# A convolution, attention and expert kernel: key deviations by Newton's steps, a new layout of the shifted rows, and new places in the slots

## The chip, the cores and the metric

The kernel runs on one core of one Trainium2 chip. A core has five engines with a queue of instructions each: TensorE (PE in the profile, its weight loads PEld), VectorE (DVE), ScalarE (ACT), GpSimd (POOL) and SyncE (SP), which here only starts DMAs. The metric is the device time of one execution in microseconds; lower is better. A matmul writes to PSUM, of which this kernel uses eight banks; everything else lies in SBUF (128 partitions) or in DRAM.

## The reference

The input x has 8 images of 56 x 56 positions with 256 channels, 25,088 tokens in all. Cut to what matters:

```python
# layer 0: 32 paths, each 256 -> 4 -> 3x3 conv -> 4 -> 256
h = relu(bn1(x @ w1 + b1)); h = relu(bn2(conv3x3(h, w2) + b2)); h = relu(bn3(h @ w3 + b3))
x = relu(sum_over_paths(h) + x)
# layer 1 on tokens t
q = layernorm(t)                                        # eps 1e-5
k = (q_head - mean) / (std(ddof=1) + 1e-5)              # per head of 32 channels; v likewise
kv = k^T v / N;  attn = q @ kv + q;  t = t + attn
z = layernorm(t)
moe = z + sum over the two best of 8 experts of weight * (gelu(z @ w1 + b1) @ w2 + b2)
out = t + moe
```

The deviations of the change's name are the std of each head and the deviation of the layer norm in front of it.

## The kernel before

The tokens are cut into S = 56 chunks of 448 tokens (8 rows of an image; NCH = 7 chunks an image). The program is a pipeline over slots s = 0, 1, ...; a slot brings together different stages of different chunks:

- conv3 of chunk s (lines 586 to 639): 16 step pairs. A pair makes two products on PE for two groups of paths (line 596, tile `c`); ACT takes one with bias and relu into a tile `r` (601), DVE takes the other and adds it into `r` (604). Every second step PE sums four of the `r` over the paths with a 0/1 matrix `gather` (617, tile `su`). There are 7 buffers of `r` and 7 PSUM banks for all products.
- conv1 of chunk s + 2 and conv2 of chunk s + 1 (255 to 339). conv2 reads `R`, the first layer's rows shifted by 0, 1 and 2 columns, which three DMAs of line 298 bring into 96 partitions; its weights `W2t` are laid out to match. Its result, split into high and low halves, goes to `hl` by DMAs (333).
- `end_steps` of chunk s - 1 (645): relu, transposes, then the keys: means per head on DVE, `center` on POOL (690), squares on ACT (699), `variances` on DVE (708 to 727) and the root of 36 values a partition by POOL's power (728), `inverse` on DVE (736 to 742), `scale` on POOL (746), and the products k^T v on PE (756).
- attention of chunk a = s - 8 (862), with its second layer norm (DVE statistics, a power on POOL at 900, or a Newton iteration on DVE at 916 for the last chunks, called alone), and its base result to the output (943).
- routing of two chunks at a time (969): scores, the two best experts, ranks, and scatters of rows into regions of DRAM by POOL (1073). At certain chunks a plan (1099) is made on DVE: which 256 rows of which expert form a tile.
- expert tiles (1252 to 1402): SP reads row and expert numbers, loads the rows `z` (1266) and the weights `w` (1276); PE transposes (1287), ACT copies, DVE copies the routing weight into `g` (1294) and the row numbers into `index` (1298); PE and ACT do the two layers (1329 to 1353), the second scaled by `g`; POOL adds the result into the output by an indirect DMA (1367).

There are 210 expert tiles. The slots have three eras: up to slot 7 only the convolution and the end steps run; from slot 8 attention and routing join; from slot 18 on tiles join. After slot 55 a tail is left, which has the last attention, routing and tiles.

The order of the work on PE, ACT and DVE is that of the program. Each step of a stage has a place between 0 and 1 in its slot, from the table `places` (1410), or it is spread evenly between two bounds; `issue` (1438) sorts a slot's steps by place and emits them. SP's and POOL's orders are left to the scheduler of the framework. `tiles_by` (1455) says how many tiles are done by each slot; its list `after` is for the slots past the last chunk.

The lines that the power and what follows it stand on:

```python
            nc.vector.tensor_scalar_mul(sd[:, :, :NH], ss, 1.0 / (HC - 1))
            nc.gpsimd.tensor_tensor(
                sd, sd, half[:T, :].rearrange("q (k h) -> q k h", k=KT), ALU.pow
            )
```

Of the kernel before, what the change touches and what calls it, by code (L numbers as in the profile page):

```python
# [8 lines left out]
F32 = mybir.dt.float32  # L9
# [16 lines left out]
def kernel(  # L26
# [165 lines left out]
    def whole(parts_of, name):  # L192
# [96 lines left out]
    def spread_taps(s):  # L289

        b, c = divmod(s, NCH)
        R = taps.tile([3 * 32, NG, TL], F32, tag="R", name=f"R_{s}")
        flat = h1.rearrange("p r w -> p (r w)")
        r0 = c * ROWS * W58
        for dx in range(3):
            n = TL - dx
            queue = nc.scalar if s == 0 and dx == 1 else nc.sync
            queue.dma_start(
                out=R[32 * dx : 32 * dx + 32, :, :n], in_=flat[:, r0 + dx : r0 + dx + n]
            )  # L300
        tapped[s] = R
# [119 lines left out]
    for f in range(NF):  # L421
        tp = ps_mm.tile([P, 512], F32, tag="mm", name=f"tp_sb_{f}")
        nc.tensor.transpose(tp[:, :NP], bias3[:, f * P : (f + 1) * P], ident[:NP, :NP])
        b3T = setup.tile([P, NP], F32, name=f"b3T_{f}")
        nc.scalar.copy(b3T, tp[:, :NP])
        nc.vector.tensor_reduce(sumb[:, f, :], b3T[:, NP // 2 :], AX.X, ALU.add)
    setup_pool.__exit__(None, None, None)
# [67 lines left out]

    b2hl = const.tile([P, C], F32R, name="b2hl")
    b2s = const.tile([P, C], F32, name="b2s")
    b2l = const.tile([E, C], F32R, name="b2l")
    nc.gpsimd.memset(b2s, 0.0)
    nc.sync.dma_start(out=b2s[:E], in_=b2)  # L500
    nc.vector.tensor_copy(b2hl, b2s)
    nc.vector.tensor_tensor(b2l, b2s[:E], b2hl[:E].bitcast(F32), ALU.subtract)
    nc.sync.dma_start(out=b2hl[E : 2 * E].bitcast(F32), in_=b2l.bitcast(F32))
# [79 lines left out]

    unit, sums = {}, {}
# [44 lines left out]
    def conv3_steps(s):  # L629
        steps = []  # L630
        units = NF * NQ
        for step in range(0, 4 * units, 2):
            if is_chunk(s):
                steps.append((0.7, lambda step=step: (pair(s, step), pair(s, step + 1))))
            if step == 0 and is_chunk(s - 1):
                steps.append((0.9, lambda: sum_paths(s - 1, units - 1)))
            if step and step % 4 == 0 and is_chunk(s):
                steps.append((0.9, lambda step=step: sum_paths(s, step // 4 - 1)))
        return steps
# [4 lines left out]

    def end_steps(s):
        b, c = divmod(s, NCH)
        v = {}

# [55 lines left out]
        def variances():  # L704
# [23 lines left out]
            nc.gpsimd.tensor_tensor(  # L728
                sd, sd, half[:T, :].rearrange("q (k h) -> q k h", k=KT), ALU.pow
            )  # L730

        def inverse():

            sd = v["sd"]
            inv = v["inv"] = small([T, KT, NH], "hinv")
            nc.vector.scalar_tensor_tensor(
                inv, sd[:, :, NH:].to_broadcast([T, KT, NH]), HEAD_EPS, sd[:, :, :NH],
                op0=ALU.mult, op1=ALU.add,
            )
# [122 lines left out]
    def attn_steps(a):  # L862
# [15 lines left out]
        def attend(k):  # L878
# [16 lines left out]
            if k == KT - 1:  # L895
                nc.vector.tensor_scalar_add(rs2, mv[:, :, 1], LN_EPS)
                if alone:
                    inverse_root(rs2)
                else:
                    nc.gpsimd.tensor_tensor(rs2, rs2, mhalf[:T, :KT], ALU.pow)  # L900
# [14 lines left out]

        def inverse_root(t):

            v, y, h = (
                stat.tile([T, KT], dt, tag=f"root{n}", name=f"root{n}_{a}", bufs=1)
                for n, dt in enumerate((F32, I32, F32))  # L920
            )
            nc.vector.tensor_copy(v, t)
            nc.vector.tensor_scalar(y, t.bitcast(I32), 1, None, ALU.arith_shift_right)
            nc.vector.tensor_scalar(y, y, -1, 0x5F3759DF, ALU.mult, ALU.add)
            y = y.bitcast(F32)
            for _ in range(4):
                nc.vector.scalar_tensor_tensor(h, y, -0.5, v, op0=ALU.mult, op1=ALU.mult)
                nc.vector.tensor_mul(h, h, y)
                nc.vector.scalar_tensor_tensor(y, h, 1.5, y, op0=ALU.add, op1=ALU.mult)
            nc.vector.tensor_copy(t, y)  # L930
# [321 lines left out]
    def empty_rows(e):  # L1252
        pad = slots.tile([P, 2, ROW], F32, tag="rows", name=f"pad_{e}")
# [27 lines left out]
    def tile_in(i):  # L1281
# [10 lines left out]

        g = slots.tile([P, 2], F32, tag="g", name=f"g_{i}")
        nc.vector.tensor_copy(g, z[:, :, C + k])  # L1294
# [92 lines left out]
    def moe_steps(first, last):  # L1387
# [20 lines left out]


    places = {  # L1410
        "attention": [0.108, 0.243, 0.378, 0.514, 0.622, 0.689, 0.744, 0.798, 0.881, 0.881],
        "attention first": [0.396, 0.487, 0.578, 0.669, 0.742, 0.834, 0.87, 0.907, 0.943, 0.989],
        "conv1": [0, 0, 0.111],
        "conv1 alone": [0, 0.011, 0.024],
        "conv2": [0.615, 0.615, 0.625, 0.675],
        "conv2 alone": [0.636, 0.642, 0.642, 0.79],
        "end": [0.109, 0.16, 0.22, 0.251, 0.346, 0.44, 0.56, 0.69, 0.77, 0.917],
        "end alone": [0.125, 0.16, 0.17, 0.23, 0.31, 0.39, 0.39, 0.64, 0.734, 0.869],
        "fetch": [0.099],
        "image": [0.012, 0.118, 0.225],  # L1420
        "plan": [0.432, 0.95],
        "route": [0.016, 0.368],
        "scatter": [0.302, 0.63],
        "taps": [0.144],
        "taps alone": [0.373],
    }

# [27 lines left out]
    def tiles_by(s):  # L1455
# [3 lines left out]
        after = [8, 5, 5, 5, 6, 5, 5, 5, 10]  # L1459
# [10 lines left out]
    for s in range(S + A + 1):  # L1470
# [17 lines left out]
        if is_chunk(a):  # L1488
# [3 lines left out]
            if a + A > S:  # L1492
                work_of.append((0.35 if opens else 0.05, 0.97, attn_steps(a)))
            else:
                work_of.extend(at("attention first" if opens else "attention", attn_steps(a)))
        work_of.extend(left)
        left = []
        if waiting and (len(waiting) == 2 or waiting[-1] % NCH == NCH - 1):
            last_image = waiting[-1] >= S - NCH
            compute, scatters = route_steps(waiting)  # L1500
            work_of.append((places["route"][0], places["route"][1], compute))
            if last_image:
                work_of.append((0.35, 1.0, sum(scatters, [])))
# [8 lines left out]
        if r >= 0 and r + 1 < len(closing):  # L1512
# [3 lines left out]
            work_of.append((0.0 if s > known_in[r] else 0.2, 1.0, moe_steps(upto, goal)))  # L1516
# [69 lines left out]
```

## Time and profile before

| | us |
|---|---|
| median of 3 runs | 3239.76 |
| lowest, highest | 3237.83, 3244.07 |
| profiled execution | 3252.06 |
| its span in the profile | 3250.3 |
| PE, DVE, ACT, POOL busy | 2947.0, 2222.2, 1923.3, 1900.3 |

The mean granted clock of TensorE was 0.959 of full speed. The profile comes from one execution and gives for each engine when each instruction ran, what ended the idle time before it, and for PE the granted clock. Line numbers are those of the kernel before. A line of a group reads: line, engine, operation, output and input tiles, shapes, count, busy us, mean ns of one, and the idle time in front with what ended it. A line of waits reads: who waited for whom, us in total, times, longest. In a timeline the two first numbers are the start and the length in us, and the bracket at the end is the idle time before it. A PE that is busy isn't a PE at its peak, since the ends of matmuls are modelled.

### The profile page before, as it was taken

The page shows a single profiled execution, that of the slowest core. Times are in us where ns is not written, and L with a number is a line of the kernel's source. Part 1 is how long each engine was busy: PE and PEld are TensorE (multiplying, and loading weights), DVE is VectorE, ACT ScalarE, POOL GpSimd, SP SyncE. Part 2 cuts the span into 40 slices and gives each one's busy share as a digit, 9 for nine tenths or more (in the row PEclk, how much of TensorE's full clock was granted, in tenths as well). Part 3 has the DMA queues.
Part 4 walks back from the last instruction along what each step waited for, and adds up shares of the span by engine and source line. Part 5 has one row for each costly group of instructions (what it writes and reads, how often), then busy time and mean ns, then how long its engine had stood idle before and what let it go on. Part 6 is the DMA issues. An engine that isn't in the chain of part 4 may idle for free. (4 is left out here: it accounts for less than half of the span.)

```text
span 3250.3 us, 53680 instructions
## 1 busy us (share of the span) xinstructions
PE 2947.0 (91%) x16677; PEld 1672.9 (51%) x16677; DVE 2222.2 (68%) x5887; ACT 1923.3 (59%) x3827; POOL 1900.3 (58%) x1372
## 2 busy tenths in 40 slices
PE   4999888888999999999899999999999998988798
PEld 2343444333454545555455555555555545776687
DVE  3778877787878787776877787877778775434210
ACT  2676655556666656566566666566666654444355
POOL 3223244445556665746656665666655757777677
PEclk7999998899999999999999999999999999989899
DMA  8442454455566766667666666667566756899797
GB/s 163 120 107 80 113 130 125 118 148 145 153 168 167 191 151 176 165 171 199 163 163 171 181 166 180 172 169 191 157 186 164 182 154 173 200 241 222 185 230 172
DMA packets 322670, 537.54 MB, mean 165 GB/s; under 512 B 41152, under 2 KB 232784, under 8 KB 322384
## 3 DMA queue, kind: packets, MB, share of 16 engines
q1 hardware_dynamic: 238272, 429.85, 46.7%
q0 software_dynamic: 81984, 103.45, 17.4%
q8 instruction: 133, 2.18, 0.3%
q10 hardware_dynamic: 2128, 0.81, 0.1%
q14 instruction: 153, 1.25, 0.1%
HBM read 248.01 MB, written 192.55 MB: 136 GB/s over the span
## 5 line engine op out<-in xcount | busy, mean ns | idle before, releaser
L604 DVE SCALAR_TENSOR_TENSOR r<-c,nb,r 128x448 f32<-128x448 f32 x1792 | 1127.5, 676 | 424.2 <-ACT r L601 380.7
L601 ACT ACTIVATE r<-c,b3t 128x448 f32<-128x448 f32 x1792 | 1040.1, 634 | 351.8 <-PE c L596 321.2
L1367 POOL DMA_INDIRECT out_dram<-y,index x420 | 661.0, 1574 | 340.1 <-ACT y L1353 206.8
L596 PE MATMUL c<-hl,W3hl 64*128 64x448 f32 x3584 | 696.1, 428 | 58.3 <-ACT r L601 20.8
L1073 POOL DMA_INDIRECT regions<-pay,rrowi x448 | 430.3, 961 | 342.8 <-PE c L596 229.5
L617 PE MATMUL su<-r,gather 128*32 128x448 f32 x3584 | 567.7, 570 | 38.2 <-DVE r L604 30.6
L596 PEld LDWEIGHTS c<-hl,W3hl 64*128 64x128 f32 x3584 | 328.8, 188 | 524.7 <-issue 247.2
L1329 PE MATMUL ph<-eT,w 128*128 128x256 f32 x1680 | 466.2, 409 | 41.0 <-DVE r L604 18.6
L1349 PE MATMUL py<-w,hT 128*128 128x256 f32 x1680 | 437.5, 385 | 2.8 <-ACT hT L1333 2.7
L1353 ACT ACTIVATE y<-py,g 128x256 f32<-128x256 f32 x420 | 196.6, 475 | 387.2 <-PE py L1349 276.2
L1329 PEld LDWEIGHTS ph<-eT,w 128*128 128x128 f32 x1680 | 307.3, 198 | 179.6 <-issue 61.2
L728 POOL TENSOR_TENSOR hsd<-hsd,half 112x36 f32<-112x36 f32 x56 | 346.6, 6189 | 85.1 <-DVE hsd L727 83.1
L1333 ACT ACTIVATE hT<-ph,w 128x256 f32<-128x256 f32 x420 | 198.1, 477 | 248.3 <-PE ph L1329 127.2
L1349 PEld LDWEIGHTS py<-w,hT 128*128 128x128 f32 x1680 | 293.9, 193 | 32.5 <-ACT hT L1333 3.5
L882 PE MATMUL at<-tab,tT 128*112 128x272 f32 x896 | 260.2, 414 | 14.2 <-ACT r L601 7.7
L690 POOL TENSOR_TENSOR norm<-t,hmean 112x512 f32<-112x512 f32 x112 | 126.8, 1259 | 240.4 <-PE c L596 130.0
L617 PEld LDWEIGHTS su<-r,gather 128*32 128x32 f32 x3584 | 100.9, 109 | 246.8 <-issue 121.9
L882 PEld LDWEIGHTS at<-tab,tT 128*112 128x112 f32 x896 | 147.3, 179 | 90.2 <-issue 21.6
L1345 PE MATMUL py<-b2hl,own 128*128 128x256 f32 x420 | 178.3, 424 | 16.6 <-issue 12.6
L1291 ACT COPY eT<-te 128x512 f32<-128x512 f32 x210 | 123.9, 590 | 85.9 <-PE te L1287 63.8
L1018 POOL TENSOR_TENSOR rq<-ebase,rq 112x8 f32<-112x8 f32 (+1 forms) x32 | 52.6, 1643 | 208.1 <-DVE rq L1017 208.1
L886 DVE SCALAR_TENSOR_TENSOR X<-at,rs,X 112x256 f32<-112x256 f32 x224 | 106.7, 476 | 80.0 <-PE at L882 36.2
(255 smaller groups left out, 3241.8 us busy)
## 6 DMA issues: line engine op xcount, KB each, us to landing
w<-Wd SPq DMA_DIRECT2D x210, 513.0 KB
rows<-regions SPq DMA_DIRECT2D x210, 259.0 KB
xi<-in_x_dram SPq DMA_DIRECT2D x56, 448.0 KB
hl<-hi SPq DMA_DIRECT2D x112, 224.0 KB
tTs<-u SPq DMA_DIRECT2D x56, 448.0 KB
ts<-t SPq DMA_DIRECT2D x56, 448.0 KB
tT<-tTs SPq DMA_DIRECT2D x56, 448.0 KB
X<-ts SPq DMA_DIRECT2D x56, 448.0 KB
```

The lines of the kernel that those rows point to most:

```text
L596: product = nc.tensor.matmul(tiles[g][:, :CH], W3hl[rows, ab, cg, :], hl[rows, ab, :], start=True, stop=True)
L601: nc.scalar.activation(r, tiles[0][:, :CH], AF.Relu, bias=b3t[:, cg, 2 * ab : 2 * ab + 1])
L604: nc.vector.scalar_tensor_tensor(r, tiles[1][:, :CH], nb3[:, cg, 2 * ab + 1 : 2 * ab + 2], r, op0=ALU.max, op1=ALU.add,)
L617: nc.tensor.matmul(ps[32 * c4 : 32 * c4 + 32, :CH], gather, unit.pop((s, 4 * u + c4)), start=(ab == 0), stop=(ab == NQ - 1),)
L728: nc.gpsimd.tensor_tensor(sd, sd, half[:T, :].rearrange("q (k h) -> q k h", k=KT), ALU.pow)
L882: nc.tensor.matmul(ps, tT[:, f, k * T : (k + 1) * T], tables_of[b][:, f, :], start=(f == 0), stop=(f == NF - 1),)
L1073: ins = nc.gpsimd.indirect_dma_start(out=regions[n], out_offset=bass.IndirectOffsetOnAxis(ap=v["row_i"][:, (m - group[0]) * KT + k, n : n ...
L1329: nc.tensor.matmul(ps, w[:, f * C + hf * P : f * C + (hf + 1) * P], eT[:, f, :], start=(f == 0), stop=(f == NF - 1),)
L1333: nc.scalar.activation(hT[:, hf, :], ps, AF.Gelu, bias=w[:, 2 * NF * C + hf : 2 * NF * C + hf + 1])
L1349: nc.tensor.matmul(ps, hT[:, f, h * P : (h + 1) * P], w[:, (NF + f) * C : (NF + f + 1) * C], start=False, stop=(f == NF - 1),)
L1353: nc.scalar.activation(y[:, h, :], ps, AF.Identity, scale=g[:, h : h + 1])
L1367: ins = nc.gpsimd.indirect_dma_start(out=out_rows, out_offset=at, in_=y[:, h, :], in_offset=None, compute_op=ALU.add, **partial,).ins
```

## The change

It has five parts.

1. From chunk 8 on (`newton = s >= 8`), `variances` doesn't call POOL's power. DVE finds 1/sqrt by a bit trick and three Newton steps (`inverse_root`, eleven instructions on 112 x 36 values) and multiplies by the value to get the root; `inverse` copies the reciprocal root of the token instead of taking a reciprocal. The Newton iteration of the last chunks' second norm uses the same function, with three steps where it had four and one copy less.
2. `R` holds the three shifts of a row in neighbouring partitions: each DMA writes every third partition of 96 instead of 32 neighbouring ones. The weights `W2s` and the mask `path32` follow; the mask is made at once, without the sum of `path96`.
3. ACT scales a tile's result by the routing weight in the loaded rows `z` themselves; the copy `g` is gone. The rows have five buffers instead of four, for the empty rows of the start too.
4. The second bias `b2` is prepared at the end of the setup, in memory that is given back after it.
5. `places` has new numbers, and names for what had fixed bounds: the attention of the last chunks, the last routing and scatters, the tiles' bounds, and `after`, whose first entry is 7 for 8.

```diff
-    path96 = setup.tile([P, 3 * GP, D], F32, name="path96")
-    group_mask(path96, 3 * GP, D, 1.0)
     path32 = setup.tile([P, GP, D], F32, name="path32")
-    nc.vector.tensor_reduce(
-        path32, path96.rearrange("q (n g) d -> q g d n", n=3), AX.X, ALU.add
-    )
+    group_mask(path32, GP, 3 * D, 1.0)
...
-                out=W2s[32 * dx : 32 * dx + 32, g],
+                out=W2s[dx : 3 * 32 : 3, g],
...
-                out=R[32 * dx : 32 * dx + 32, :, :n], in_=flat[:, r0 + dx : r0 + dx + n]
+                out=R[dx : 3 * 32 : 3, :, :n], in_=flat[:, r0 + dx : r0 + dx + n]
...
+    def inverse_root(v, y, h):
+
+        nc.vector.tensor_scalar(y, v.bitcast(I32), 1, None, ALU.arith_shift_right)
+        nc.vector.tensor_scalar(y, y, -1, 0x5F3759DF, ALU.mult, ALU.add)
+        y = y.bitcast(F32)
+        for _ in range(3):
+            nc.vector.scalar_tensor_tensor(h, y, -0.5, v, op0=ALU.mult, op1=ALU.mult)
+            nc.vector.tensor_mul(h, h, y)
+            nc.vector.scalar_tensor_tensor(y, h, 1.5, y, op0=ALU.add, op1=ALU.mult)
+        return y
...
-            nc.gpsimd.tensor_tensor(
-                sd, sd, half[:T, :].rearrange("q (k h) -> q k h", k=KT), ALU.pow
-            )
+            if not newton:
+                nc.gpsimd.tensor_tensor(
+                    sd, sd, half[:T, :].rearrange("q (k h) -> q k h", k=KT), ALU.pow
+                )
+                return
+            y = stat.tile([T, KT, NH + 1], I32, tag="root1", name=f"root1_{s}", bufs=1)
+            h = stat.tile([T, KT, NH + 1], F32, tag="root2", name=f"root2_{s}", bufs=1)
+            y = v["y"] = inverse_root(sd, y, h)
+            nc.vector.tensor_mul(sd, sd, y)
...
-            nc.vector.reciprocal(rs1s[s], sd[:, :, NH])
+            if newton:
+                nc.vector.tensor_copy(rs1s[s], v["y"][:, :, NH])
+            else:
+                nc.vector.reciprocal(rs1s[s], sd[:, :, NH])
...
-        z = slots.tile([P, 2, ROW], F32, tag="rows", name=f"rows_{i}")
+        z = slots.tile([P, 2, ROW], F32, tag="rows", name=f"rows_{i}", bufs=5)
...
-        g = slots.tile([P, 2], F32, tag="g", name=f"g_{i}")
-        nc.vector.tensor_copy(g, z[:, :, C + k])
+        g = z[:, :, C + k]
...
-        "attention first": [0.396, 0.487, 0.578, 0.669, 0.742, 0.834, 0.87, 0.907, 0.943, 0.989],
+        "attention first": [0.396, 0.487, 0.578, 0.669, 0.742, 0.953, 0.953, 0.953, 0.953, 0.989],
-        "conv2": [0.615, 0.615, 0.625, 0.675],
+        "conv2": [0.615, 0.615, 0.655, 0.675],
-        "conv2 alone": [0.636, 0.642, 0.642, 0.79],
+        "conv2 alone": [0.607, 0.613, 0.613, 0.761],
-        "end": [0.109, 0.16, 0.22, 0.251, 0.346, 0.44, 0.56, 0.69, 0.77, 0.917],
+        "end": [0.109, 0.151, 0.211, 0.242, 0.337, 0.431, 0.551, 0.681, 0.761, 0.908],
-        "image": [0.012, 0.118, 0.225],
+        "image": [0.001, 0.107, 0.214],
-        "plan": [0.432, 0.95],
+        "plan": [0.569, 0.983],
-        "route": [0.016, 0.368],
+        "route": [0, 0.368],
-        "scatter": [0.302, 0.63],
+        "scatter": [0.302, 0.551],
-        "taps alone": [0.373],
+        "taps alone": [0.391],
...
-                work_of.append((0.35 if opens else 0.05, 0.97, attn_steps(a)))
+                work_of.extend(at("attention first last" if opens else "attention last", attn_steps(a)))
...
-            work_of.append((0.0 if s > known_in[r] else 0.2, 1.0, moe_steps(upto, goal)))
+            work_of.append((places["tiles"][s <= known_in[r]], places["tiles"][2], moe_steps(upto, goal)))
```

Of what is left out above: the tiles' bounds are now 0.043 (0.2 in the first slot of a round) to 0.99, the last image's routing stands at 0 to 0.254, its scatters from 0.35 to 0.995, fetch at 0.119 (0.099 before).

More of the change, by code (lines that the diff above doesn't have):

```diff
@@ L426 @@
         nc.vector.tensor_reduce(sumb[:, f, :], b3T[:, NP // 2 :], AX.X, ALU.add)
+    b2hl = const.tile([P, C], F32R, name="b2hl")
+    b2s = setup.tile([P, C], F32, name="b2s")
+    b2l = setup.tile([E, C], F32R, name="b2l")
+    nc.gpsimd.memset(b2s, 0.0)
+    nc.sync.dma_start(out=b2s[:E], in_=b2)
+    nc.vector.tensor_copy(b2hl, b2s)
+    nc.vector.tensor_tensor(b2l, b2s[:E], b2hl[:E].bitcast(F32), ALU.subtract)
+    nc.sync.dma_start(out=b2hl[E : 2 * E].bitcast(F32), in_=b2l.bitcast(F32))
     setup_pool.__exit__(None, None, None)
@@ L494 @@
     Wd = tc.dram_tile([E, P, WROW], F32, name="Wd")
[L496 to L503, printed above, removed]
     pos_i = const.tile([P, 2], I32, name="pos_i")
@@ L578, in unordered @@
         tc.declare_no_dep(ins, group=group, keep=keep, reason="other rows")
+    places = {
+        "after": [7, 5, 5, 5, 6, 5, 5, 5, 10],
+        "attention": [0.108, 0.243, 0.378, 0.514, 0.622, 0.689, 0.744, 0.798, 0.881, 0.881],
+        "attention first": [0.396, 0.487, 0.578, 0.669, 0.742, 0.953, 0.953, 0.953, 0.953, 0.989],
+        "attention last": [
+            0.151, 0.272, 0.393, 0.514, 0.611, 0.611, 0.657,
+            0.706, 0.754, 0.791, 0.815, 0.839, 0.863, 0.912,
+        ],
+        "attention first last": [
+            0.611, 0.692, 0.774, 0.856, 0.921, 0.962, 0.982,
+            0.982, 0.982, 0.982, 0.982, 0.982, 0.982, 0.982,
+        ],
+        "conv1": [0, 0, 0.111],
+        "conv1 alone": [0, 0.011, 0.024],
+        "conv2": [0.615, 0.615, 0.655, 0.675],
+        "conv2 alone": [0.607, 0.613, 0.613, 0.761],
+        "end": [0.109, 0.151, 0.211, 0.242, 0.337, 0.431, 0.551, 0.681, 0.761, 0.908],
+        "end alone": [0.143, 0.178, 0.188, 0.248, 0.328, 0.408, 0.408, 0.658, 0.752, 0.887],
+        "fetch": [0.119],
+        "image": [0.001, 0.107, 0.214],
+        "tiles": [0.043, 0.2, 0.99],
+        "conv3": [0.7, 0.9],
+        "plan": [0.569, 0.983],
+        "route": [0, 0.368],
+        "route last": [0, 0.254],
+        "scatter": [0.302, 0.551],
+        "scatter last": [0.35],
+        "taps": [0.144],
+        "taps alone": [0.391],
+    }
     unit, sums = {}, {}
@@ L633, in conv3_steps @@
             if is_chunk(s):
-                steps.append((0.7, lambda step=step: (pair(s, step), pair(s, step + 1))))
+                steps.append((places["conv3"][0], lambda step=step: (pair(s, step), pair(s, step + 1))))
             if step == 0 and is_chunk(s - 1):
-                steps.append((0.9, lambda: sum_paths(s - 1, units - 1)))
+                steps.append((places["conv3"][1], lambda: sum_paths(s - 1, units - 1)))
             if step and step % 4 == 0 and is_chunk(s):
-                steps.append((0.9, lambda step=step: sum_paths(s, step // 4 - 1)))
+                steps.append((places["conv3"][1], lambda step=step: sum_paths(s, step // 4 - 1)))
         return steps
@@ L647, in end_steps @@
         v = {}
+        newton = s >= 8
         def begin():
@@ L897, in attend @@
                 if alone:
-                    inverse_root(rs2)
+                    y, h = (
+                        stat.tile(
+                            [T, KT, NH + 1], dt, tag=f"root{n}", name=f"root{n}_{a}_a", bufs=1
+                        )[:, :, 0]
+                        for n, dt in ((1, I32), (2, F32))
+                    )
+                    nc.vector.tensor_copy(rs2, inverse_root(rs2, y, h))
                 else:
@@ L914, in normed @@
             )
[L916 to L930, printed above, removed]
         def raised(k):
@@ L1252, in empty_rows @@
     def empty_rows(e):
-        pad = slots.tile([P, 2, ROW], F32, tag="rows", name=f"pad_{e}")
+        pad = slots.tile([P, 2, ROW], F32, tag="rows", name=f"pad_{e}", bufs=5)
         nc.gpsimd.memset(pad, 0.0)
@@ L1402, in moe_steps @@
         return steps
-    places = {
-        "attention": [0.108, 0.243, 0.378, 0.514, 0.622, 0.689, 0.744, 0.798, 0.881, 0.881],
-        "attention first": [0.396, 0.487, 0.578, 0.669, 0.742, 0.834, 0.87, 0.907, 0.943, 0.989],
-        "conv1": [0, 0, 0.111],
-        "conv1 alone": [0, 0.011, 0.024],
-        "conv2": [0.615, 0.615, 0.625, 0.675],
-        "conv2 alone": [0.636, 0.642, 0.642, 0.79],
-        "end": [0.109, 0.16, 0.22, 0.251, 0.346, 0.44, 0.56, 0.69, 0.77, 0.917],
-        "end alone": [0.125, 0.16, 0.17, 0.23, 0.31, 0.39, 0.39, 0.64, 0.734, 0.869],
-        "fetch": [0.099],
-        "image": [0.012, 0.118, 0.225],
-        "plan": [0.432, 0.95],
-        "route": [0.016, 0.368],
-        "scatter": [0.302, 0.63],
-        "taps": [0.144],
-        "taps alone": [0.373],
-    }
     def at(name, steps):
@@ L1458, in tiles_by @@
         most = known_after[-2] - 2
-        after = [8, 5, 5, 5, 6, 5, 5, 5, 10]
+        after = [int(v) for v in places["after"]]
         if s >= S:
@@ L1500 @@
             compute, scatters = route_steps(waiting)
-            work_of.append((places["route"][0], places["route"][1], compute))
+            rt = places["route" if s < S else "route last"]
+            work_of.append((rt[0], rt[1], compute))
             if last_image:
-                work_of.append((0.35, 1.0, sum(scatters, [])))
+                work_of.append((places["scatter last"][0], 0.995, sum(scatters, [])))
             else:
```

## The prediction

> **What bounds the kernel now.** I read the page first (engine totals, the forty slices), then a table by stage, then who waited for whom in each stage, then a timeline of one wait. The stage borders are the first relu of line 601 of a slot: slots 0 to 7 (convolution alone) 65 to 335 us, slots 8 to 18 (attention and routing join) to 814, slots 19 to 55 (expert tiles join) to 2717, then the tail without convolution, whose last part (3124 on) has tiles only. Columns: stretch, its length, busy us of PE, its weight loads, DVE, ACT, POOL with counts, granted PE clock, DMA share, GB/s.
>
> ```profile
> PE 2947.0 (91%) x16677; PEld 1672.9 (51%) x16677; DVE 2222.2 (68%) x5887; ACT 1923.3 (59%) x3827; POOL 1900.3 (58%) x1372
> ...
> 65.00:335.30 270.30, 252.21 (x1478) 108.08 (x1476) 211.84 (x401) 181.50 (x324) 71.68 (x35) 0.99 0.42 110
> 335.30:814.40 479.10, 412.46 (x2367) 187.48 (x2366) 379.49 (x933) 284.69 (x544) 225.12 (x154) 0.93 0.49 130
> 814.40:2717.00 1902.60, 1800.09 (x10475) 982.67 (x10474) 1454.28 (x3681) 1204.23 (x2395) 1192.55 (x812) 0.98 0.66 171
> 2717.00:3124.00 407.00, 342.81 (x1665) 279.41 (x1666) 144.67 (x728) 177.23 (x413) 288.48 (x215) 0.92 0.86 212
> 3124.00:3250.00 126.00, 114.63 (x600) 100.94 (x598) 12.16 (x77) 68.85 (x142) 97.41 (x64) 0.96 0.81 194
> ```
>
> PE is 95% busy in the long third stage, so there only its gaps and its lowered clock can be won. The second stage is different: PE idles 66.6 us of 479 and the clock is lowest. The waits of DVE and PE in that stage, then in the third (us in total, times, longest):
>
> ```profile
> DVE hinv L736 <- POOL hsd L728: 26.3, 9, 4.2
> PE su L617 <- DVE r L604: 27.0, 10, 4.2
> ...
> DVE hinv L736 <- POOL hsd L728: 36.9, 30, 3.2
> PE kv L756 <- DVE r L604: 23.0, 10, 4.4
> PE ph L1329 <- DVE r L604: 18.6, 11, 2.1
> ```
>
> The two totals of the second stage are one event, as slot 10 shows: POOL's power takes 6.16 us, DVE stands 4.22 us in front of it, the relus behind stand too, and PE stands 4.21 us.
>
> ```profile
> 442.80 6.16 POOL L728 TENSOR_TENSOR hsd<-hsd,half 112x36 f32<-112x36 f32 x1
> 449.00 0.19 DVE L736 SCALAR_TENSOR_TENSOR hinv<-hsd 112x32 f32<-112x32 f32 x1 [4.22 <-POOL hsd L728]
> 450.24 1.70 PE L617 MATMUL su<-r,gather 128*32 128x448 f32 x3 [4.21 <-DVE r L604]
> ...
> 450.20:454.60 4.40, 4.36 (x13) 1.49 (x13) 2.45 (x5) 1.36 (x3) 2.75 (x3) 0.50 0.09 28
> ```
>
> The last line is the stretch after it: PE runs at half its clock. In the third stage the waits have another cause:
>
> ```profile
> L728 POOL TENSOR_TENSOR hsd<-hsd,half 112x36 f32<-112x36 f32 x56 | 346.6, 6189 | 85.1 <-DVE hsd L727 83.1 <-DVE hmu L723 0.9 <-issue 0.9
> L1294 DVE COPY g<-rows 128x2 f32<-128x2 f32 x210 | 72.5, 346 | 27.2 <-ACT y L1353 18.8 <-issue 8.4
> ...
> 1132.42 3.06 DVE L1294 COPY g<-rows 128x2 f32<-128x2 f32 x1
> 1132.80 2.65 POOL L690 TENSOR_TENSOR norm<-t,hmean 112x512 f32<-112x512 f32 x2
> 1136.20 1.13 PE L1329 MATMUL ph<-eT,w 128*128 128x256 f32 x4 [2.05 <-DVE r L604]
> ```
>
> A copy of two columns, 0.16 us in the median of 210, lasts 3.06 us while POOL centers the keys, and PE then stands 2.05 us.
>
> [...] GpSimd's power does not seem to block (the cast at line 328 took 0.38 us inside slot 10's). [...] In the trace's packet records between 1000 and 2600 us a packet of R (2,312 bytes, into 32 neighbours) has a median of 214 ns, one of 3,584 bytes for u and t 140 ns[...].
>
> **The change, part by part.**
>
> *Newton on DVE, chunks 8 to 55.* Removed: 48 powers of 6.19 us, 297 us of POOL. Added on DVE: two tensor_scalars, nine steps and a product, 12 instructions in a chain. The like-sized chain of lines 714 to 723 starts one every 0.22 us (durations 0.19), so 12 x 0.22 = 2.6 us a chunk, 48 x 2.6 = 125 us; the reciprocal of rs1 (0.12) becomes a copy (0.16), nothing. Behind the chain on DVE stand u, the relus and hi and lo; PE's sums wait for the relus. Second stage, ten chunks: the 27.0 us of PE waits go. Half clock behind them is 37.5 us by the clock records of slots 10 to 17, which lost up to 18.8 us; I take 10. Against that the chain is exposed: slot 9 has 1.8 us of idle DVE between variances and inverse to absorb 2.6, others less; exposure 0.9 to 2.6, taken as 1.5, ten times 15. Sum -22; ends -27 - 18.8 + 9 = -37 and -27 + 26 = about 0. Third stage, 37 chunks: the 36.9 us of DVE waits cost PE only 2 us by its own waits, and slots are filled by tiles, so the chain mostly runs beside ph and py: credit -5, exposure 0.2 us x 37 = +7. If that cover is gone, 2 us x 37 = +74. Sum +2; ends -15, +74. In slots 19 to 55 DVE has 448 us idle against 37 x 2.6 = 96 added.
>
> *Weights without a copy.* 210 copies go, 72.5 us of DVE, about half of it blocked time. [...] PE's ph waits are 18.6 us, and the half clock at slots 25, 27, 34, 41 and 53 is 5 x 3.41 us, costing half: 8.5. Ends -27 and 0; I take -11. The rows buffer is now held until ACT has scaled with it (line 1353), two iterations longer, with five buffers for four: taking rows n + 2 waits for output n - 3, which is the last step of the iteration before. SP's weight load n + 1 has waited for that same output all along (480.8 us of SP wait at line 1276), so SP's queue gets no new bound; rows still have two iterations of 4.1 us before they are turned. Cost 0; without the cover, up to the tail's DMA-heavy 400 us x 2%, 8 us.
>
> *Shifted rows over all partitions.* If R's packets fell to the rate of the 3,584-byte ones, 90 ns, DMA work between 1000 and 2600 would fall by 12,032 packets x (199 mean - 90) / 16 = 82 us, five points of share. No PE gap over 0.8 us in slots waits for R, and conv2 stands 0.47 of a slot (22 us) behind taps: 0, ends -8, +3. The mask in one piece saves one reduce of 0.27 us, hidden under W2's loads.
>
> *b2 into the setup.* One memset, two DMAs, two DVE instructions move ahead by a little; PE waits there for g3's DMA (10.8 us). 0.
>
> *New places.* The order of PE's instructions stays, but for the last third of conv2 (one pair-step later), the image matrix before conv1, and tiles, which start at 0.043 of a slot and come 3 or 4 a slot more evenly; one tile moves from the tail into the slots (4.1 us either way). The plan moves from 0.432-0.95 to 0.569-0.983. Its long DVE instructions were blocked behind POOL in slots 26, 33, 47 and 54 (2.76 and 2.88 us in a row in slot 26) and PE waited 4.4 us at kv each time, 23.0 us in all, with 4 x 6.83 us at half clock: 37 us at stake. Later, they meet the POOL sum X instead of the scale: I take a third, -12; ends -37, +10. Tail: PE idles 64 us of 407 before 3124, at clock 0.92. Route and attention come earlier, so scatters and last plan can too: -5; ends -40, +20 (DMA is at 0.86 there). Newton with three steps instead of four in seven tail chunks: 0.7 us each on a DVE that is 36% busy, 0.
>
> Sum: -22 + 2 - 11 - 12 - 5 = -48 us on the profiled 3252.06 us (span 3250.3): 3204. The runs' median is 3239.76, 12.3 below the profiled one: **3192 us**.
>
> **Rivals.** *More is won* (0.20): the kv and ph waits go whole and the tail fills; -37 + 2 - 27 - 30 - 20 = -112, 3128 us. For: the waits are few, with a place each. [...] *The waits only move* (0.10): [...] plan collides with the sum X, the exposed chain eats what the power's wait cost; 0 to -12, 3228 to 3240. *DVE's chain becomes the bound* (0.17), slower: variances already hold DVE 2.5 us in a row and would hold it 5.1; the relu ring has 7 buffers, and slot 9 shows a DVE hold of 2.25 us reaching PE as 2.24. At 2 us exposed in 37 slots and 2.6 in ten the sum is -48 + 67 + 11 = +30, 3270 us. It decides where the exposure exceeds my values by 1.0 us a chunk on the mean (48/47). Against: DVE is 76% busy in the third stage and PE has tiles to run. The change not taking effect is excluded for Newton, since the instructions are there; for R it is in the third rival.
>
> **How the numbers follow.** The forecast has 0.53, own range 3165 to 3222. To hold eight in ten the range takes in half of the larger gain and the moved waits and the near part of the slower case: 3140 to 3255. A measurement tells 0.2%, 6.5 us, from no change. Slower: 0.17 plus a bit of the moved waits, 0.18; same 0.05; faster 0.77.
>
> **What would show it.** No power at line 728 beyond 8; POOL about 1600 us busy; DVE about 2270 (2222 + 125 - 72.5 - 5). In the second stage the wait of su for r falls from 27 us to under 15, and the clock rises from 0.93. The L1298 copies keep a mean under 0.25 us. kv's wait in the third stage falls by a third. PE's relu waits rising in every slot after line 727's place would prove the prediction wrong, as would SP waiting for ACT at the rows load with te waiting for rows, or a tail longer than 533 us.

## The result and the profile after

The changed kernel took **3205.92 us** in the median of 4 runs (3205.22 to 3206.05), the kernel before 3240.41 beside it: a ratio of 0.9892, interval [0.9875, 0.9909]. The profiled execution took 3205.89 us, its span is 3204.2, the granted clock 0.969 in the mean. In a later group of runs (`after_b` below) the same kernel took 3236.3 beside 3247.5 us, ratio 0.9957 [0.9943, 0.9971]. The change is a gain both times, of 34 us and of 11.

The busy totals from the page of the changed kernel, and the group of the index copy before and after (columns as in the prediction):

```profile
PE 2932.1 (92%) x16677; PEld 1660.9 (52%) x16677; DVE 2282.0 (71%) x6224; ACT 1917.9 (60%) x3827; POOL 1600.1 (50%) x1324
...
L1298 DVE COPY index<-rows 128x2 int32<-128x2 int32 x180 | 34.4, 192 | 71.0 <-DMA out_dram<-y,index 70.8
L1336 DVE COPY index<-rows 128x2 int32<-128x2 int32 x180 | 67.6, 376 | 124.3 <-DMA out_dram<-y,index 107.0 <-issue 17.2
```

POOL lost 300 us of work and DVE gained 60 net. The copy `g` is gone, yet the index copy behind it, which took 34.4 us, now takes 67.6: 2 of its 180 executions lasted over 0.5 us before, 22 do now. The stages of the changed kernel, with the columns of the prediction's table: convolution alone, slots 8 to 18, slots 19 to 55, tail.

```profile
61.40:334.90 273.50, 250.30 (x1478) 105.62 (x1476) 214.46 (x401) 181.52 (x324) 72.89 (x35) 0.99 0.36 108
334.90:801.40 466.50, 404.50 (x2369) 183.22 (x2370) 397.82 (x1051) 286.43 (x544) 163.00 (x144) 0.95 0.44 133
801.40:2688.70 1887.30, 1807.61 (x10496) 980.81 (x10496) 1499.62 (x4007) 1203.11 (x2400) 964.08 (x777) 0.98 0.65 173
2688.70:3204.20 515.50, 442.36 (x2240) 374.28 (x2240) 149.42 (x698) 240.03 (x549) 375.50 (x275) 0.95 0.86 214
```

Against before (65.0, 270.3, 479.1, 1902.6 and 533.0 us) the start gave 3.6, the second stage 12.6, the third 15.3 and the tail 17.5 us, and the first stage took 3.2. What PE waited for in the second stage, and below the dots in the third:

```profile
PE su L646 <- DVE u L653: 20.7, 8, 2.6
PE su L646 <- DVE r L633: 4.0, 5, 1.7
...
PE sv L841 <- DVE Arow L840: 16.6, 10, 2.1
PE kv L806 <- DVE r L633: 12.3, 11, 2.0
PE su L646 <- DVE u L653: 9.9, 18, 1.4
```

The 27.0 us that PE stood for the relus behind POOL's power in the second stage are down to 4.0, but 20.7 have come that were not there: PE stands for `u`, the instruction that follows the Newton chain on DVE. Slot 10 after, to be read beside slot 10 in the prediction:

```profile
443.96 2.88 PE L646 MATMUL su<-r,gather 128*32 128x448 f32 x8 [2.60 <-DVE u L653]
```

So PE's idle time hardly fell in that stage, from 66.6 to 62.0 us. What fell is the time at half clock: by the trace's clock records it was 68.5 us before and is 48.5 now, and PE is busy 8.0 us less for the same work. In the third stage kv's wait fell from 23.0 to 12.3 us, ph's 18.6 us for a relu are gone, and the wait for `u` is new. (The wait of `sv` belongs to the matrix of an image; it was 12.4 us before.)

This leaves two theories. *Stages*: Newton pays in slots 8 to 18 and costs in the third stage, and the new places bring the gain. *Sum as forecast*: Newton is a gain overall, about nothing in the third stage, and the places bring little.

### The profile page after: what moved, and what is told of

It is laid out like the page before. It is cut to its first block, busy times and chain, and to the rows that moved or that the text cites. A ratio compares the mean times of both kernels' runs of the same rounds, so it can differ in the third digit from the quotient of the medians.

```text
span 3204.2 us, 54123 instructions
## 1 busy us (share of the span) xinstructions
PE 2932.1 (92%) x16677; PEld 1660.9 (52%) x16677; DVE 2282.0 (71%) x6224; ACT 1917.9 (60%) x3827; POOL 1600.1 (50%) x1324
## 3 DMA queue, kind: packets, MB, share of 16 engines
q0 software_dynamic: 81984, 103.45, 17.5%
## 5 line engine op out<-in xcount | busy, mean ns | idle before, releaser
L1391 ACT ACTIVATE y<-py,rows 128x256 f32<-128x256 f32 x420 | 195.8, 475 | 478.2 <-PE py L1387 371.7
L1367 PE MATMUL ph<-eT,w 128*128 128x256 f32 x1680 | 451.4, 400 | 18.8 <-DMA w<-Wd 9.3
L796 POOL TENSOR_TENSOR norm<-norm,hinv 112x512 f32<-112x512 f32 x112 | 123.2, 1172 | 151.7 <-DVE rs L790 78.5
L967 ACT ACTIVATE pay<-X,nm,rs 112x256 f32<-112x256 f32 x224 | 132.5, 602 | 70.8 <-DVE nm L960 66.8
L1383 PEld LDWEIGHTS py<-b2hl,own 128*128 128x128 f32 x420 | 79.8, 190 | 156.8 <-issue 47.0
```

Source lines behind the costliest of these rows:

```text
L1367: nc.tensor.matmul(ps, w[:, f * C + hf * P : f * C + (hf + 1) * P], eT[:, f, :], start=(f == 0), stop=(f == NF - 1),)
L1383: nc.tensor.matmul(ps, own.to_broadcast([P, P]), b2hl, start=True, stop=False)
L1391: nc.scalar.activation(y[:, h, :], ps, AF.Identity, scale=g[:, h : h + 1])
```

## The experiments

Stage lengths of every run, in us, worked out in the same way: from the first relu of slots 0, 8 and 19 and the last of slot 55. Runs between two lines were made together on one chip: the last three groups on three different ones, called the second, third and fourth group here. The record doesn't say which chip the first pair had.

| run | start | 0 to 7 | 8 to 18 | 19 to 55 | tail | span |
|---|---|---|---|---|---|---|
| before | 65.1 | 270.2 | 479.1 | 1902.4 | 533.5 | 3250.3 |
| after | 61.4 | 273.5 | 466.5 | 1887.4 | 515.4 | 3204.2 |
| --- | | | | | | |
| before_b | 66.1 | 269.4 | 481.1 | 1893.7 | 534.6 | 3244.8 |
| no_newton | 67.4 | 272.1 | 482.8 | 1845.3 | 535.5 | 3203.2 |
| newton_late | 65.8 | 273.0 | 470.7 | 1865.0 | 533.2 | 3207.7 |
| places_old | 66.0 | 270.1 | 473.2 | 1937.2 | 535.9 | 3282.5 |
| --- | | | | | | |
| after_b | 64.7 | 273.4 | 467.1 | 1904.1 | 529.0 | 3238.3 |
| newton_mid | 64.8 | 273.5 | 466.4 | 1852.1 | 527.0 | 3183.6 |
| index_act | 66.3 | 272.6 | 466.1 | 1892.3 | 529.1 | 3226.4 |
| r_old | 67.1 | 272.1 | 466.3 | 1896.7 | 530.0 | 3232.1 |
| --- | | | | | | |
| newton_only | 65.3 | 269.3 | 469.4 | 1939.3 | 528.8 | 3272.2 |
| g_back | 63.1 | 272.2 | 466.1 | 1904.1 | 525.6 | 3231.1 |
| tail_old | 61.8 | 273.4 | 466.4 | 1887.4 | 529.6 | 3218.6 |
| best | 63.4 | 270.2 | 467.7 | 1848.1 | 533.2 | 3182.6 |

Diffs are against the changed kernel, unless said.

**Before and after once more.** `before_b` and `after_b` are the two kernels unchanged, in the second and the third group.

> The kernel before again, unchanged, for a second profile. Its profiled execution of 3252.06 us lay 12 us above its median. If that is spread of the tail (DMA and the order of the indirect sums), the stage from 2717 us on is shorter here and the stages up to slot 55 end within 2 us of the first profile; if it is spread everywhere, every stage shrinks by the same 0.4%.

> The changed kernel again, unchanged, beside the next three. Its first profile had a tail of 515.4 us where five other profiles, three of them with the same tail, have 533 to 536, and a start of 61.4 us where they have 65 to 67. If that is the chip or its hour, the tail is 533 to 536 here, and the stages of slots 8 to 55 are within 2 us of 466.5 and 1887.4. If it belongs to the changed kernel, the tail is 515 again.

Measured: 3246.51 us (one run) and 3236.3 (median of 9, 3227.18 to 3241.03; before beside it 3247.51). Neither expectation came true as written. The spread of the kernel before was in its third stage (1902.4 and 1893.7 us), not in its tail; the changed kernel's tail lay between the two values named, and its third stage was 1904.1 us where 1887.4 stood. The slots that differ most are the plan's 26, 33, 40 and 47, with 52.8 to 53.1 us in `after` and 54.4 to 54.7 in `after_b`, and slot 43 with 56.2 and 61.7. `r_old` below, with the same order of instructions on PE, DVE and ACT, has the longer value in some of these slots and the shorter in others, and 1896.7 us in all. What picks one is open. So a difference of under 17 us between two profiles' third stages says nothing here, and the start (61 to 67 us) and the tail (515 to 536) vary too, in kernels that are alike there.

**No Newton for the keys, all else changed.**

```diff
-        newton = s >= 8
+        newton = False
```

> The changed kernel with POOL's power kept for all chunks. Theory (Newton pays only where DVE used to stand for POOL in slots 8 to 18): that stage grows from 466.5 us by 10 to 15 us, the stage of slots 19 to 55 changes by less than 5, sum 3216 to 3226 us. Rival (the places alone made the gain and Newton's chain costs as much as the power's wait): within 6 us of 3206. Rival (POOL's relief pays everywhere): 3240 or more.

Measured: 3207.8 us beside 3250.24 before, ratio 0.9875 [0.9858, 0.9891]. Without its leading part the change gains no less: the total is that of the first rival, and the third stage moved far more than the theory had it. Its second and third stage, and the waits in the second:

```profile
339.50:822.30 482.80, 422.16 (x2369) 194.34 (x2370) 376.56 (x933) 286.27 (x544) 225.49 (x154) 0.90 0.42 128
822.30:2667.60 1845.30, 1783.24 (x10496) 976.28 (x10496) 1397.03 (x3563) 1200.47 (x2400) 1196.32 (x814) 0.98 0.67 177
```

```profile
PE su L646 <- DVE r L633: 25.1, 10, 3.5
DVE hinv L783 <- POOL hsd L770: 23.2, 9, 3.5
```

In the second stage the power's wait is back and the stage is 16 us longer than in the changed kernel, at clock 0.90 in place of 0.95. PE's idle time is the same in both (60.6 and 62.0 us): waits of up to 3.5 us stand against waits of 2.6, and 99.0 us at half clock against 48.5. So what Newton wins here shows in the clock and hardly in PE's idle time. The third stage is 42 us shorter than the changed kernel's shorter length. Both signs of *Stages* show here, though `after` may have run on another chip.

**Newton in slots 8 to 17 alone.**

```diff
-        newton = s >= 8
+        newton = 8 <= s < 18
```

> The changed kernel with Newton for chunks 8 to 17 only and POOL's power before and after. Theory (the chain pays while DVE stands for POOL in slots 9 to 18, and costs where tiles and plans fill DVE): second stage 466 to 470 us as in the changed kernel, third 1843 to 1850 as without Newton, so 35 to 45 us faster than the changed kernel beside it. Rival (the third stage of the run without Newton was short for another reason, such as the phase in which it was entered): third stage above 1870, gain under 15 us.

Measured: 3186.02 us beside 3247.51, ratio 0.9809 [0.9783, 0.9835]; the changed kernel on that chip took 3236.3. The second stage keeps its 466.4 us, the third loses 52:

```profile
804.60:2656.70 1852.10, 1783.96 (x10496) 978.18 (x10496) 1404.21 (x3563) 1200.62 (x2400) 1195.76 (x814) 0.98 0.66 176
```

The rival is excluded, and this separates the stages on one chip. POOL has 230 us more to do there than in after_b and DVE 98 less, and PE is done 52 us earlier. Slot by slot 20 of the 52 us lie in the plan's slots 26, 33, 40 and 47, and 5 in slot 43. Slot 26, from the table by stretch, first in after_b, then in newton_mid:

```profile
1159.20:1213.90 54.70, 50.11 (x287) 27.00 (x288) 47.44 (x138) 32.28 (x66) 26.38 (x22) 0.97 0.60 154
```

```profile
1150.80:1199.00 48.20, 46.94 (x285) 25.51 (x285) 44.18 (x125) 32.13 (x66) 31.19 (x23) 1.00 0.68 178
```

The timeline of after_b in that slot shows what the chain does (start, length, engine and line, idle time in front):

```profile
1188.06 0.18 DVE L677 TENSOR_SCALAR root<-root 112x36 int32<-112x36 int32 x1
...
1190.35 0.20 DVE L777 TENSOR_TENSOR hsd<-hsd,root 112x36 f32<-112x36 f32 x1
1190.47 0.68 DVE L653 SCALAR_TENSOR_TENSOR u<-su,sumb,xT 128x448 f32<-128x448 f32 x1
1191.20 0.95 PE L646 MATMUL su<-r,gather 128*32 128x448 f32 x4 [0.45 <-DVE u L653]
...
1198.39 2.39 DVE L1223 TENSOR_TENSOR big<-iot,qi 128x112 f32<-128x112 f32 x1
1198.57 2.07 POOL L796 TENSOR_TENSOR norm<-norm,hinv 112x512 f32<-112x512 f32 x2
...
1202.69 2.19 POOL L981 TENSOR_TENSOR X<-X,pay 112x1024 f32<-112x1024 f32 x1 [0.30 <-ACT pay L967]
1203.10 1.81 DVE L1237 SCALAR_TENSOR_TENSOR run<-iot,run 128x14 f32<-128x14 f32 x1
1205.85 3.29 PE L806 MATMUL kv<-norm 112*128 112x129 f32 x16 [1.95 <-DVE r L633]
```

The chain holds DVE for 2.7 us (1187.84 to 1190.55) and what is behind it comes later. Two of the plan's instructions then run beside POOL's scale and sum and take 2.39 and 1.81 us, where they last 0.27 and 0.17 in slot 26 of newton_mid; the relus behind are late and kv waits 1.95 us (0.45 in newton_mid). In newton_mid two other instructions of the plan last long beside the same two of POOL, 1.53 us beside the scale and 2.78 beside the sum, and what this adds comes to 3.8 us in both runs, so it doesn't make the difference. What holds these instructions isn't shown. What is left is the chain's own time on DVE and the order in which things meet behind it; the two aren't told apart here. The other 27 us are spread over the slots: 28, 35, 42 and 49 lose 1.3 to 1.9 us each, 24, 31, 38, 45 and 52 1.0, 23 and 30 some 0.4. PE's idle time accounts for 16 of the 52, most of it waits for `u` (9.9 us in 18 slots, none in newton_mid) and for relus (7.3 against 0.8), and the clock lost 7 us more. The rest shows as longer records of matmuls (the sums `su` +12.3 us, conv3 +6.7), whose ends are modelled, so how it divides further stays open.

**Newton's chain later.** The chain gets its own step after `variances`, at 0.64 of a slot, where it stood at 0.551 with it.

```diff
-        "end": [0.109, 0.151, 0.211, 0.242, 0.337, 0.431, 0.551, 0.681, 0.761, 0.908],
+        "end": [0.109, 0.151, 0.211, 0.242, 0.337, 0.431, 0.551, 0.64, 0.681, 0.761, 0.908],
...
-            (1.0, center), (0.6, squares), (1.8, variances), (0.8, inverse), (0.8, scale),
+            (1.0, center), (0.6, squares), (1.8, variances), (0.5, roots), (0.8, inverse), (0.8, scale),
```

> The changed kernel with Newton's chain as a step of its own at place 0.64, behind the sum u and the relus that PE waits for, instead of straight after the variances. Theory (the chain stands in front of u on DVE, and PE waits for u's bank, 2.6 us a slot in slots 9 to 17 and about 0.5 after): PE's wait of su for u, 20.7 us in the second stage and 9.9 in the third, nearly goes; 15 to 35 us faster, 3171 to 3191. Rival (DVE is full there, so the 2.6 us come back at the next sum): the wait moves to su for r, time within 6 us of 3206.

Measured: 3208.81 us beside 3250.24, ratio 0.9869 [0.9852, 0.9885], the time that the rival named. PE's waits for `u` are gone in both stages, but su waits for the relus instead (10.3 us in 11 times in the second stage, 17.2 in 17 in the third), as the rival had it, and the second stage takes 470.7 us, 4 more. The third takes 1865.0: 22 to 39 less than the changed kernel's, and still 20 more than without Newton on the same chip. So a part of the cost is where the chain stands, a part is that it is there.

**All places as before, the other parts changed.** The old table, bounds and list of `after`.

```diff
-        "plan": [0.569, 0.983],
+        "plan": [0.432, 0.95],
...
-        "end": [0.109, 0.151, 0.211, 0.242, 0.337, 0.431, 0.551, 0.681, 0.761, 0.908],
+        "end": [0.109, 0.16, 0.22, 0.251, 0.346, 0.44, 0.56, 0.69, 0.77, 0.917],
```

> The changed kernel with the old places everywhere, the old list of tiles by slot and the old bounds of the last attention, routing and scatters. Theory (places made the gain of the stage of slots 19 to 55 and of the tail): 25 to 35 us slower than the changed kernel, 3231 to 3241, with the first stage back from 273.5 to about 270 us and the slots of plans (26, 33, 47, 54) back at 56 to 58 us. Rival (Newton, the rows and the copy made it): within 10 us of 3206.

Measured: 3279.53 us, ratio 1.0082 [1.0065, 1.0099]: slower than before, and outside what both theories gave. Its first stage is back at 270.1 us, its third is 1937.2, 33 to 50 more than in the changed kernel; ph's wait for a relu is back at 18.1 us in 12 times. The places without the chain stand in no_newton and before_b, both of this group: kv's wait falls there from 21.7 to 3.9 us, ph's from 18.3 to none, PE's idle time from 103.6 to 62.1, and the third stage by 48 us.

**Newton in the kernel before.** The kernel before with Newton's steps for the keys from chunk 8 on, and nothing else:

```diff
+            if s < 8:
+                nc.gpsimd.tensor_tensor(
+                    sd, sd, half[:T, :].rearrange("q (k h) -> q k h", k=KT), ALU.pow
+                )
+                return
+            y = stat.tile([T, KT, NH + 1], I32, tag="yroot1", name=f"yroot1_{s}", bufs=1)
+            h = stat.tile([T, KT, NH + 1], F32, tag="yroot2", name=f"yroot2_{s}", bufs=1)
+            y = v["y"] = key_root(sd, y, h)
+            nc.vector.tensor_mul(sd, sd, y)
```

> The kernel before with Newton's steps for chunks 8 to 55 and nothing else of the change. Theory (the chain pays in slots 9 to 18 and costs more after them, in the old places as in the new): 15 to 40 us slower than before, with a second stage of 470 to 475 us and a third of 1925 to 1945. Rival (Newton is only harmful beside the new places): within 8 us of before.

Measured: 3276.54 us beside 3245.3, ratio 1.0092 [1.0071, 1.0112]. The second stage gains 10 to 12 us, the third loses 37 to 46. Its waits of PE in the third stage:

```profile
PE ph L1349 <- DVE r L604: 18.6, 11, 2.0
...
PE su L617 <- DVE u L624: 15.3, 19, 2.2
PE kv L776 <- DVE r L604: 10.5, 9, 2.2
```

ph's waits for relus are still there, kv's are halved, and the one for `u` has come on top. So the chain costs its time in the old places as in the new ones. g_back, on the same chip, differs from this kernel in the places, R, b2 and the shorter iteration of the tail, and takes 43 us less; R is worth nothing (below), so the places are worth about that.

**The copy back.** The copy `g` and four row buffers again.

```diff
-        z = slots.tile([P, 2, ROW], F32, tag="rows", name=f"rows_{i}", bufs=5)
+        z = slots.tile([P, 2, ROW], F32, tag="rows", name=f"rows_{i}")
...
-        g = z[:, :, C + k]
+        g = slots.tile([P, 2], F32, tag="g", name=f"g_{i}")
+        nc.vector.tensor_copy(g, z[:, :, C + k])
```

> The changed kernel with the copy g on DVE again and four buffers of rows instead of five. Theory ([...] the copy itself is all that is saved): DVE busy grows by 210 x 0.16 to 0.2, 34 to 42 us, not by 72; the third stage is within 8 us of the changed kernel's (1887 to 1904), 1890 to 1912. Rival (the copy removed was worth the 11 us of the prediction or more): third stage 1915 or more.

Measured: 3233.68 us (3223.12 to 3238.44) beside 3245.3, ratio 0.9953 [0.9935, 0.9972]; after_b had 0.9957. The copy's removal is worth no time that can be told, and ph's wait for a relu is absent here too, so it was the places that took it away. The groups of the two copies:

```profile
L1333 DVE COPY g<-rows 128x2 f32<-128x2 f32 x210 | 73.8, 352 | 68.7 <-ACT y L1392 35.0 <-issue 30.1 <-ACT X L974 3.6
...
L1337 DVE COPY index<-rows 128x2 int32<-128x2 int32 x180 | 36.9, 205 | 35.6 <-DMA out_dram<-y,index 34.7 <-issue 0.8
```

Both together take 110.7 us; in the changed kernel the index copy alone takes 67.6. Of the 73.8 us removed, 31 were taken over by the next instruction, whose mean went from 205 to 376 ns. DVE's busy total is only 11.5 us above the changed kernel's (2293.8 and 2282.3 in after_b), less than the 34 to 42 expected: the records of short instructions overlap, so a copy's record is longer than what it adds. In before a record of `g`, 0.16 us long in the median, begins 0.08 us before the one in front of it ends, and the next begins 0.09 before it ends (medians of 210).

**The index copy on ACT.**

```diff
-            nc.vector.tensor_copy(index, z[:, :, C + 2].bitcast(I32))
+            nc.scalar.copy(index, z[:, :, C + 2].bitcast(I32))
```

> The changed kernel with the copy of the row numbers on ACT instead of DVE. Theory ([...] 37 us of its 67 us are waiting behind POOL, and DVE is what plan slots wait for): DVE busy falls by about 60 us, ACT rises by 180 copies of 0.2 us, the third stage gets 10 to 25 us shorter. Rival (those copies stand where PE has other work): third stage within 5 us of the changed kernel's. In the tail DVE no longer stands for the indirect sums; ACT does, and PE needs ACT for every tile, so the tail may be up to 20 us longer.

Measured: 3231.75 us (3221.86 to 3242.81), ratio 0.9955 [0.9936, 0.9974], not to be told from after_b's. On ACT it takes 37.2 us, 207 ns each, the longest 257: none is lengthened. DVE's busy total fell by 48.4 us (about 60 expected), and no other instruction on DVE grew by more than 2.2 us in all, so this time the lengthening was not handed on. The third stage of the profiled execution was 1892.3 us, between the two lengths of the changed kernel, so nothing is shown of it. The tail, at 529.1 us, is that of after_b (529.0): ACT does not lengthen it.

**R as before.**

```diff
-                out=R[dx : 3 * 32 : 3, :, :n], in_=flat[:, r0 + dx : r0 + dx + n]
+                out=R[32 * dx : 32 * dx + 32, :, :n], in_=flat[:, r0 + dx : r0 + dx + n]
```

> The changed kernel with the shifted rows in three blocks of 32 partitions again, and the weights and the mask to match. Theory (no step waits for R): within 4 us of the changed kernel beside it, while R's packets take about 40 us more of DMA engine time between 1000 and 2600 us. Rival (DMA work saved comes back as earlier rows and weights): 5 to 15 us slower, in the third stage or the tail.

Measured: 3235.68 us (18 runs), ratio 0.9966 [0.9957, 0.9976]; after_b 3236.3. The packets of 2,312 bytes had a median of 233 ns between 1000 and 2600 us, 156 ns in after_b. Those of the unshifted rows (2,320 bytes) had 100 in r_old, into 32 neighbours as well, and 94 in after_b. So the 32 neighbours alone don't make a packet slow, and the prediction, which compared the 2,312-byte packets, saw only a part of it. The transfers are faster, and no idle time in front of the matmuls that read `R` is put down to them, in before or in after.

**The tail as before.** Old first entry of `after`, old bounds of the last attention, routing and scatters.

```diff
-        "after": [7, 5, 5, 5, 6, 5, 5, 5, 10],
+        "after": [8, 5, 5, 5, 6, 5, 5, 5, 10],
-        "route last": [0, 0.254],
+        "route last": [0.016, 0.368],
```

> The changed kernel with the old work of the tail: last attention spread over 0.05 to 0.97, last routing at 0.016 to 0.368, scatters to 1.0, and 8 as the first of the tiles after the last chunk. Theory (the tail of 515 us in the first profile belonged to the chip, since the changed kernel's tail was 529 on the second): the tail is within 5 us of those of the three kernels beside it that have the new one. Rival (the new tail is worth the difference between 533 and 515): 10 to 20 us longer.

Measured: 3224.53 us (3220.3 to 3237.31) beside 3245.3. The tail takes 529.6 us. On the same chip newton_only, with the old tail too, has 528.8, and the new tail took 525.6 (g_back) and 533.2 (best). In the second group the new tail took 533.2 and 535.5, the old 534.6 and 535.9. So no gain of the tail's new places can be told, and the 18 us in the first pair of profiles aren't shown to be theirs.

**A version of what paid.** Newton in slots 8 to 17, the old places in the first stage, the index copy on ACT.

```diff
-        "conv2 alone": [0.607, 0.613, 0.613, 0.761],
+        "conv2 alone": [0.636, 0.642, 0.642, 0.79],
-        "end alone": [0.143, 0.178, 0.188, 0.248, 0.328, 0.408, 0.408, 0.658, 0.752, 0.887],
+        "end alone": [0.125, 0.16, 0.17, 0.23, 0.31, 0.39, 0.39, 0.64, 0.734, 0.869],
-        "taps alone": [0.391],
+        "taps alone": [0.373],
-        newton = s >= 8
+        newton = 8 <= s < 18
-            nc.vector.tensor_copy(index, z[:, :, C + 2].bitcast(I32))
+            nc.scalar.copy(index, z[:, :, C + 2].bitcast(I32))
```

> Newton for chunks 8 to 17 only, the row numbers copied on ACT, and the old places of the first era. Theory (each acts in its own stage): the first stage falls from 273 to 270 us, the second stays at 466 to 470, the third falls below the 1852 us of Newton for chunks 8 to 17 alone by 0 to 12; 3165 to 3185 us, and 2% below the kernel before beside it. Rival (ACT is needed in the tail for every tile): the tail grows by 5 to 20 us and eats it.

Measured: **3177.74 us** (3173.35 to 3184.69) beside 3245.3, ratio 0.9781 [0.976, 0.9802]: the fastest of all, 2.2% below before. Its interval overlaps newton_mid's, so what it adds to that is shown in the first stage alone. Its tail of 533.2 us is 4 to 8 longer than the others of its group, as the rival had it, but index_act's was not, so this may be spread. The first and the third stage:

```profile
63.40:333.60 270.20, 252.08 (x1478) 108.13 (x1476) 211.92 (x401) 181.27 (x324) 71.65 (x35) 0.99 0.37 109
...
801.30:2649.40 1848.10, 1789.17 (x10497) 978.59 (x10496) 1365.66 (x3444) 1208.81 (x2519) 1194.00 (x814) 0.98 0.66 176
```

The first stage is back at 270.2 us. In the changed kernel its new places had put `lo` beside POOL's scale. The group of `lo` in slots 0 to 7, in before and in after:

```profile
L329 DVE TENSOR_TENSOR lo<-h,hi 128x448 fp32r<-128x448 f32 x8 | 5.0, 626 | 0.3
```

```profile
L325 DVE TENSOR_TENSOR lo<-h,hi 128x448 fp32r<-128x448 f32 x8 | 10.1, 1261 | 0.3
```

## Why the forecast came out near

The forecast was 3192 us and 3205.9 was measured, within its own range of 3165 to 3222. The sum stood at -48 us on the profiled run, 3252.06, and -46 came (3205.89). The nearness is luck. The terms did not come as written: two large errors, of opposite sign, cancelled. And it holds for the first pair alone: in `after_b` the same kernel took 3236.3 us, outside that range, and gained 11 us of 48.

- **Newton in the second stage, -22.** Measured -12.6 in the first pair, -11.7 in newton_only against before_b (another chip), -16.3 in after against no_newton. The mechanism was right, and the credits came nearly whole: the waits for relus fell by 23.0 of their 27.0 us, and half clock by 20.0 us, which is the 10 us that the prediction took. The mis-sized term is the exposure. It was taken as 1.5 us in ten chunks, and PE waits 2.6 us for `u` in eight of them, the upper end that the prediction named: 20.7 us where 15 stood. -23.0 - 10.0 + 20.7 makes -12.3. What one gap costs in clock can't be read from one slot. In slot 10 the old gap of 4.21 us goes with 10.24 us at half clock, begun inside the gap, and the new one of 2.60 us is followed by 3.41; but the old gaps of 4.2 us in slots 12, 14 and 17 go with 3.41 us, and the new one of 2.57 us in slot 13 with none. Nearly all records of half clock are 3.41 us long or a multiple of it (44 of 45 in before, 35 of 36 in after).
- **Newton in the third stage, +2.** This is the step that failed: "the chain mostly runs beside ph and py", exposure 0.2 us a chunk. Measured +35 to +52 (after and after_b against newton_mid; newton_only against before and before_b +37 to +46), which is 1.0 to 1.4 us a chunk over 37. The tiles gave little cover: `u` and the relus stand behind the chain in DVE's order, and PE's sums wait for them between the tiles (9.9 us for `u` in 18 slots of after). The slower rival had this mechanism, with 2 us a chunk, and was to win where the exposure exceeded the values taken by 1.0 us; it did so by about that much, but the places covered it.
- **Weights without a copy, -11.** Measured 0. "The L1298 copies keep a mean under 0.25 us" was wrong: 0.376 (line 1336 of the changed kernel). The credit rested on ph's waits, which went with the places (none in g_back, which has the copy). The rival that the waits only move fits the copies, where 31 us passed to the next one. (In the prediction's lines the long copy is recorded from 1132.42 to 1135.48 us and POOL's centering from 1132.80 to 1135.45, so they show the two side by side, and not what holds the copy.) The cover named for the held rows was right, since nothing was lost either.
- **R, 0.** Right: 3235.7 and 3236.3. The DMA time of R between 1000 and 2600 us, a sixteenth of its packets' sum, fell by 40 us from before to after (48 from r_old to after_b) where the author's estimate from the rate of the 3,584-byte packets was 82; it was off the path.
- **New places, -12.** The other mis-sized term: -33 to -50 in the third stage (places_old against after and after_b; no_newton against before_b gives -48). A third of what hangs on kv's wait had been credited; without the chain that wait fell from 21.7 to 3.9 us, and ph's 18.3 us went as well. Together these are 36 of the 48 us. In the changed kernel, with the chain, kv's wait is 12.3 us.
- **First stage, 0.** Measured +3.3, in the same slots where `lo` stands beside POOL's scale and lasts 0.7 us longer; with the old places of these slots both are gone (best), and which of the moved steps is to blame isn't shown. The prediction did not treat the places of the slots without attention.
- **Tail, -5.** No gain can be told. The 17.5 us of the first pair are mostly the execution's or the chip's, and so may be the 3.6 of the start.
- **Busy totals.** POOL 1600 as forecast, DVE 2282 for 2270: the index copies took 33 us more than forecast, the chain 13 less (112 for 125), and other instructions 8 less.

In the third group the parts make: -14 (second stage, against before_b) - 48 (places, from the second group) + 52 (Newton in the third) + 4 (first) = -6 us; -11 were measured. In the first pair the third stage was at its shorter length and the tail short as well.

## What to carry to other kernels

Moving work from an idle engine to the one that feeds the critical engine paid only in the stage where that engine waited for the idle one: here the same chain was worth 12 to 16 us in eleven slots and cost 35 to 52 in the next thirty-seven. When a short instruction that is long beside another engine's work is taken away, look at the one behind it: here the next copy grew from 205 to 376 ns in the mean, and the lengthening was gone only when that one had left the engine too; neither step gained time that could be told. When a change comes with new places, run each part without the other: the places hid a loss as large as their gain, and leaving out most of the named change gave the faster kernel.

## What the runs showed of the hardware that was not expected

- The lengthening passed on: index copy 205 ns in the mean behind `g`, 376 without it, 207 on ACT.
- A VectorE subtraction `lo` of 128 x 448 takes 0.63 us alone and 1.35 beside POOL's scale (seven of the eight in slots 0 to 7).
- No `lo` is longer beside POOL's power, which takes 6.2 us on the two tiles `hsd` and `half`: 40 of the 56 `lo` in before lie wholly inside a power, and none of them took more than 0.63 us. As far as `lo` shows, the power cost DVE only the wait for its result.
- A gap of 2.60 us on PE was followed by 3.41 us at half clock, and one of 2.57 us three slots later by none.
- The same kernel gave a third stage of 1887.4 and of 1904.1 us, and in the tail, where the DMA share is 0.84 to 0.86, 515.4 and 529.0 us.
